# A graph layer on one core: the turn back of a chunk as a product with two stacked identities, one Vector step on GpSimd, and a new order of all work

## The chip, the cores and the metric

One core of a Trainium2 chip runs the kernel. The metric is the device time of one execution in microseconds; the engines are PE (TensorE), DVE (VectorE), ACT (ScalarE), POOL (GpSimd) and SP (SyncE), which issues the loads here. Six runs of the kernel before have a median of 193.21 us (192.71 to 194.0).

## The reference, cut to what matters

```python
h = relu(layernorm(x))                       # x: 4096 x 64
support = h @ weight                         # 64 x 64
mask = (adj != 0)                            # adj: 4096 x 4096, float32, 64 MiB
rank = cumsum(mask, axis=1); deg = rank[:, -1:]
k = minimum(deg, 100); pos = rank - (deg - k)
w = mask * where(pos > 0, 0.5 ** (k - pos), 0)
out = x + w @ support + bias
```

In each row the last 100 neighbours count, and a neighbour weighs half as much for each further neighbour that stands to the right of it.

## The kernel before, in words

The 32 row tiles (128 rows each) are taken in 8 chunks of four. Each chunk is two units: the right half of its columns first, then the left half. So there are 16 units (0 to 15) of four tiles, 64 tiles (0 to 63), and each tile is one load of 1 MB into one of 8 buffers (`a_sb`, issued by SP on line 120). Load n waits for the conversion of tile n-8, which frees its buffer.

For each tile: `convert` (line 341, DVE) turns floats to bytes; for the tiles in the tuple `signed` it is done on ACT instead (line 339). `transpose` (line 352, PE) makes four 128x128 transposes, and `settle` (line 363, DVE) copies them out of PSUM into the unit's mask. For each unit: `totals` (line 369, PE) counts bits; `split` (line 379, ACT) and `divide` (line 382, DVE) each take one byte plane of the counts out of PSUM; `carry` (line 388, POOL, units with an odd number only) brings over the count of the unit to the right; `suffix` (line 396, PE) and `clamp` (line 400, DVE) make the number of later neighbours. Then for each half of the unit's eight blocks, `place` (lines 407 and 412, PE) makes exponents in four PSUM banks out of five; `weigh` (line 420, ACT) takes the exponential of one block, and `aggregate` (line 457, PE) multiplies it with the support, which is held as a rounded part and a remainder, side by side in 64 + 64 columns (`hr`). So the accumulator `acc` has 128 partitions, 64 for either part.

Three late blocks, called `QUICK`, (14, 4), (15, 0) and (15, 4), pass by ACT: `encode` (line 426, DVE) makes an exponent code out of PSUM, `cut` (line 431, DVE) adds a constant to it, `take` (line 435, DVE) rounds it into the weight, and `gather` is their `aggregate`, with a scaled copy of the support that `lower` (line 443, POOL) has made. The last three blocks of unit 15 are weighed and multiplied in two halves (`PARTED`).

At the end of a chunk: `drain` (line 473, ACT) brings `acc` to SBUF and adds the bias; `turn_back` (line 480, PE) transposes it in four 128x128 pieces into the PSUM tile `po`; `finish` (lines 487 and 488, DVE) adds first the one 64-column part and then the other to x. The last chunk does this in two halves, with the second drain on DVE (line 471). Stores follow, on SP (lines 490 and 495) and one on ACT's queue.

The order of the work is written by a planner (lines 531 to 655): each step is a task with an engine, a rank (a place in the stream plus the numbers of `shift` and `own`), a booked cost and the tasks that it needs. The planner picks the task with the lowest rank among those that can start within `wait` of the earliest, and the steps are then issued in the order of their planned starts. Every engine keeps that order, which is fixed in the program (lines 666 to 672). The semaphores between engines follow from the data alone.

Of the kernel before, what the change touches and what calls it, by code (L numbers as in the profile page):

```python
# [31 lines left out]
def kernel(  # L32
# [134 lines left out]
    nc.vector.memset(less, 0.0)  # L167
    ones = setup.tile([P, H], F32, name="ones")
# [159 lines left out]
    low, codes, masks, words, wts, accs, tots, pts, sums8, behind, vs, signed = {}, {}, {}, {}, {}, {}, {}, {}, {}, {}, {}, (2, 8)  # L328
# [100 lines left out]
    def cut(u, k):  # L429

        nc.vector.tensor_scalar(codes[u, k][:, 1].bitcast(I32), codes[u, k][:, 0].bitcast(I32), 100 * 2.0 ** 23, None, op0=ALU.add)
# [43 lines left out]
    def turn_back(g, part=None):  # L475
        if ("o", g) not in pts:
            pts["o", g] = ps_t.tile([P, TG, 2, D], F32, tag="t", name="po")
        n = TG if part is None else TG // 2
        for tt in range(n):
            nc.tensor.transpose(pts["o", g][:, (part or 0) * n + tt, :, :].rearrange("p s d -> p (s d)"),  # L480
                                sums[g, part][:, tt * P:(tt + 1) * P], ident)

    def finish(g, part=None):
        r = slice(0, TG) if part is None else slice(part * TG // 2, (part + 1) * TG // 2)
        t = slice(g * TG % HT + r.start, g * TG % HT + r.stop)
        o = xr[:, g * TG // HT, t, :]
        nc.vector.tensor_add(o, pts["o", g][:, r, 0, :], o)
        nc.vector.tensor_add(o, pts["o", g][:, r, 1, :], o)
        if part is not None:
            (nc.sync if part else nc.scalar).dma_start(out_v[:, g * TG // HT, t, :], o)  # L490

    def store(r):
# [8 lines left out]
    shift = {"aggregate": 45, "carry": -26.5, "center": 25, "clamp": -23.5, "constants": 43.5, "convert": 36, "cut": 18.5,  # L501
             "divide": 0.5, "drain": -44.5, "encode": -1, "finish": -29.5, "first": -47.5, "halved": 5, "lower": 10.5,
             "order_of": 19.5, "power": -19.5, "relu": 39.5, "root": 26.5, "scale": 31, "second": 23.5, "settle": -26,
             "split": -38.5, "spread": 12, "square": 48.5, "store": 8, "suffix": 25, "support": 70, "take": -12, "totals": -32,
             "transpose": -15.5, "turn": 20, "turn_back": 62, "turned": 29, "weigh": 24}
    own = {
           "aggregate": {(0, 0): 6, (0, 3): -2, (0, 4): -16, (0, 6): -11, (1, 0): 7, (1, 1): -18, (1, 5): -5, (1, 7): -9, (11, 4): 10, (11, 5): 14, (11, 6): 6, (11, 7): -1, (12, 0): -20, (12, 3): 4, (12, 4): -2, (12, 5): -4, (12, 6): -10, (13, 1): -10, (13, 2): 6, (13, 3): 8, (13, 4): 1, (13, 5): -12, (13, 6): -4, (13, 7): -12, (14, 0): 2, (14, 1): 1, (14, 2): -16, (14, 3): -11, (14, 4): 15, (14, 5): -8, (14, 6): 18, (14, 7): -36, (15, 2): -4, (15, 3): -2, (15, 4): 1, (15, 5): 1, (15, 5, 0): -1, (15, 5, 1): -6, (15, 6): 8, (15, 6, 0): 7, (15, 6, 1): -3, (15, 7): -2, (2, 1): 4},
           "carry": {(1,): -2, (13,): 6, (15,): 3, (3,): 29}, "center": {(0,): 1, (1,): 2, (2,): 1, (3,): 3},
           "clamp": {(0,): -13, (1,): -8, (13,): 7, (15,): -14, (2,): -8, (3,): -2}, "constants": {(0,): -17, (1,): 15},
           "convert": {(1,): 20, (12,): -12, (13,): 4, (14,): -4, (16,): 19, (17,): 8, (18,): -16, (19,): -4, (2,): -9, (20,): -1, (4,): 5, (5,): 9, (57,): -16, (58,): -5, (59,): 8, (6,): -1, (60,): -5, (61,): -1, (7,): 1, (8,): 16, (9,): 8},  # L510
           "count": {(2,): 1}, "counted": {(2,): -18, (4,): 8}, "cut": {(14, 4): 15},
           "divide": {(0,): 24, (1,): 2, (14,): 8, (15,): -14, (2,): 15, (3,): -4},
           "drain": {(0,): 8, (5,): -22, (6,): 6, (7, 0): 7, (7, 1): 4}, "encode": {(14, 4): -9},
           "finish": {(5,): 7, (6,): -33, (7, 0): 4, (7, 1): -1}, "first": {(0, 0): -1, (1, 0): 1, (1, 1): 8},
           "halved": {(0,): -3, (1,): -5, (13,): 4, (14,): -9, (2,): 4}, "lower": {(15, 0): -3}, "order_of": {(2,): 4, (4,): 3},
           "place": {(0, 0): -8, (0, 1): -8, (1, 0): -13, (12, 1): 1, (13, 0): 8, (13, 1): -2, (14, 0): -9, (14, 1): 5, (15, 0): -26, (15, 1): 2, (2, 0): -4, (2, 1): 16},
           "power": {(): -23}, "relu": {(0,): -4, (1,): -3, (2,): 8}, "root": {(): -7}, "scale": {(3,): -6},
           "second": {(0, 0): -6, (0, 1): -1, (1, 1): 22},
           "settle": {(1,): -4, (10,): 2, (11,): 1, (12,): -9, (13,): 19, (15,): 2, (17,): -2, (18,): -19, (19,): -6, (2,): -11, (3,): 6, (4,): -11, (5,): -4, (56,): 5, (57,): 22, (58,): -2, (59,): 5, (6,): 1, (61,): -4, (63,): -4, (9,): 1},
           "split": {(0,): 5, (1,): -9, (13,): 3, (14,): 9, (15,): 3, (2,): -1, (3,): -12},  # L520
           "spread": {(0,): 10, (1,): 14, (2,): -9, (3,): -1}, "square": {(1,): 10, (2,): -5, (3,): -12},
           "store": {(0,): -13, (1,): -3}, "suffix": {(1,): 3, (13,): -36, (14,): -6, (15,): -1}, "support": {(0,): -3, (2,): 15},
           "take": {(15, 0): -4, (15, 4): -2},
           "totals": {(0,): -1, (1,): -4, (13,): 3, (14,): -4, (15,): 10, (2,): -2, (3,): 7, (4,): -15},
           "transpose": {(0, 0, 2): 4, (0, 2, 4): -9, (1, 0, 2): -8, (10, 0, 2): -16, (11, 0, 2): 7, (11, 2, 4): 14, (12, 0, 2): -2, (12, 2, 4): -18, (13, 0, 2): -1, (13, 2, 4): 4, (14, 0, 2): -16, (15, 0, 2): -1, (15, 2, 4): 5, (16, 2, 4): -14, (17, 0, 2): -12, (18, 0, 2): 29, (18, 2, 4): 29, (19, 0, 2): 16, (19, 2, 4): -4, (2, 0, 2): -2, (2, 2, 4): 1, (3, 2, 4): -15, (4, 0, 2): 3, (4, 2, 4): 21, (5, 0, 2): -4, (5, 2, 4): -4, (56, 0, 2): 1, (56, 2, 4): -1, (57, 0, 2): -27, (58, 0, 2): 1, (58, 2, 4): 8, (59, 0, 2): 5, (6, 0, 2): 25, (6, 2, 4): 37, (60, 2, 4): -7, (61, 0, 2): 10, (61, 2, 4): 6, (63, 0, 2): -8, (7, 0, 2): -2, (8, 0, 2): -1, (8, 2, 4): -16, (9, 2, 4): -1},
           "turn": {(0, 0): -12, (0, 12): 10, (0, 4): 2, (0, 8): 3, (1, 0): -25, (1, 4): -16},
           "turn_back": {(5,): 4, (6,): -22, (7, 0): 8}, "turned": {(0, 0): 2, (0, 12): 6, (1, 12): -6, (1, 4): 12, (1, 8): 14},
           "weigh": {(0, 2): 8, (0, 3): 3, (0, 4): 3, (0, 5): 4, (0, 7): -16, (1, 0): 22, (1, 3): -3, (1, 4): 1, (1, 7): 2, (12, 3): 8, (12, 4): -8, (12, 5): -6, (12, 6): -22, (12, 7): 6, (13, 0): 2, (13, 1): -12, (13, 2): 23, (13, 5): 10, (13, 6): -8, (13, 7): 5, (14, 3): -3, (14, 5): -4, (14, 7): -8, (15, 2): -4, (15, 3): -11, (15, 5, 0): 3, (15, 5, 1): -19, (15, 6): 7, (15, 6, 0): -3, (15, 6, 1): -4, (15, 7): -5, (15, 7, 0): 4, (15, 7, 1): 3, (2, 0): 2, (2, 1): 4, (2, 3): -7, (2, 4): 8, (2, 6): 2, (2, 7): -1, (3, 0): -4, (3, 1): 1}}
# [50 lines left out]
    for u, (g, c0, cb) in enumerate(UNITS):  # L579
# [3 lines left out]
        task(divide, (u,), DVE, at - 2.5, 600, 720, [("totals", u)])  # L583
# [5 lines left out]
        for k in range(2 * cb):  # L589
# [7 lines left out]
            if (u, k) in QUICK:  # L597
                weighs = "take"
                task(encode, (u, k), DVE, due - 8, 1150, 1270, [("place", u, k // 4), ("convert", NT - 2)])
                task(cut, (u, k), DVE, due - 8, 650, 770, [("encode", u, k)])  # L600
                task(take, (u, k), DVE, due - 8, 650, 770, [("cut", u, k)], ("w", ("gather", u, k)))
# [5 lines left out]
        for part in range(2 if u == U - 1 else 0):  # L607
            for k in PARTED:
                due = at + k + part
                task(weigh, (u, k, part), ACT, due + 2.5, 520, 650, [("place", u, k // 4)], None if part else ("w", ("aggregate", u, k, 1)))  # L610
                task(aggregate, (u, k, part), PE, due + 14, 260, 500, [("weigh", u, k, part)])
        if c0 == 0:
            at = POS[(u + 1) * TG]
            if u < U - 1:
                task(drain, (g,), ACT, at, 560, 620, [("aggregate", u, 2 * cb - 1)] + ([("turn_back", g - 1)] if g else []))
                task(turn_back, (g,), PE, at + 5, 440, 660, [("drain", g)], ("t", ("finish", g)))
                task(finish, (g,), DVE, at + 2, 820, 880, [("turn_back", g)])
            else:
                for part in range(2):
                    task(drain, (g, part), DVE if part else ACT, at, 300, 350, [("aggregate", u, PARTED[-1], part), *(("gather", *uk) for uk in QUICK)])  # L620
                    task(turn_back, (g, part), PE, at + 5, 220, 440, [("drain", g, part)])
# [79 lines left out]
```

## Time and profile before

| | us |
|---|---|
| median of six runs | 193.21 |
| the profiled execution | 193.93 |
| its span, first to last instruction | 192.2 |
| busy: PE, DVE, ACT, POOL | 173.1, 165.8, 158.1, 19.7 |
| landing of the last load (tile 63) | 167.76 |
| convert of tile 63 | 169.66 to 171.04 |
| first `weigh` of unit 15 | 179.50 |
| last `aggregate` ends | 186.73 |
| last store is issued | 189.56 |

The span is counted from the first instruction; what lies around it in this execution is 1.7 us. The view of the stretches gives each engine's busy time in a part of the span; the timeline gives single instructions with start, duration and, in brackets, the idle time before them and who ended it. "DVE L363" is an instruction of line 363 on DVE. Busy PE time is modelled from pipelined matmuls and overstates PE. DVE and ACT instructions in a row overlap by about 0.1 us, so one `convert` of 1.39 us takes 1.27 us of a queue that is full, and one `weigh` of 1.12 us takes 1.02.

### The profile page before, as it was taken

How to read it: one execution, taken by the hardware profiler on the slowest of the kernel's cores; microseconds unless marked ns; L12 is line 12 of the kernel's file. 1: busy time of each engine (PE TensorE's matmuls, PEld its weight loads, DVE VectorE, ACT ScalarE, POOL GpSimd, SP SyncE). 2: the span in 40 equal slices, each digit the busy share in tenths (PEclk: the TensorE clock that was granted, in tenths of full speed). 3: DMA queues.
4: the chain of work that ended last, by engine and by line, in shares of the span. 5: the costliest groups of instructions: out<-in, count | busy, mean ns of one | idle time of the engine just before them, and what ended most of it. 6: DMA issues, size and time to landing. Idle time of an engine off the chain costs nothing.

```text
span 192.2 us, 3811 instructions
## 1 busy us (share of the span) xinstructions
PE 173.1 (90%) x1504; PEld 107.1 (56%) x1504; DVE 165.8 (86%) x225; ACT 158.1 (82%) x175; POOL 19.7 (10%) x60
## 2 busy tenths in 40 slices
PE   7699998787997999999999989999999898989981
PEld 5577958353664556555665645655565454544460
DVE  4853876999998999899989988999999999988753
ACT  2289109999798799979996999999999699998880
POOL 7000053100001000100010002000100048001000
PEclk9999759997999999999999999999999999999996
DMA  6999999999999999999999999999999999602000
GB/s 218 419 421 419 419 424 421 418 416 416 426 411 424 421 418 423 423 414 426 419 414 423 423 418 419 426 414 423 414 419 418 423 419 419 270 6 82 0 3 27
DMA packets 10338, 69.49 MB, mean 362 GB/s; under 512 B 1360, under 2 KB 1616, under 8 KB 2128
## 3 DMA queue, kind: packets, MB, share of 16 engines
q1 hardware_dynamic: 10016, 69.15, 87.0%
q8 instruction: 12, 0.20, 0.4%
q10 hardware_dynamic: 304, 0.10, 0.2%
q14 instruction: 6, 0.05, 0.1%
HBM read 68.19 MB, written 1.05 MB: 360 GB/s over the span
## 4 chain that ended last, share of the span: by engine, by line
PE 43%; DVE 19%; issue 16%; ACT 13%; POOL 7%; POOLq 0%; ACTq 0%; DVEq 0%
PE acc L457 15%; ACT wk L420 11%; PE pt L352 8%; DVE m L341 8%; PE v L412 4%; DVE mt L363 4%; PE v L407 3%; PE tot L369 3%; POOL low L443 3%; PE pd L281 2%; PE pc L265 2%; PE ps L396 2%; PE px L256 2%; DVE sums L382 1%; DVE xs L307 1%
## 5 line engine op out<-in xcount | busy, mean ns | idle before, releaser
L420 ACT ACTIVATE wk<-v,floor 128x1024 fp32r<-128x1024 uint8 (+1 forms) x128 | 130.1, 1100 | 14.7 <-PE v L412 14.5
L341 DVE TENSOR_SCALAR m<-a_sb 128x2048 uint8<-128x2048 f32 x62 | 86.3, 1394 | 2.5 <-DMA a_sb<-in_adj_dram 2.5
L457 PE MATMUL acc<-wk,hr 128*128 128x512 f32 (+1 forms) x256 | 79.4, 425 | 1.5 <-ACT acc_sb L473 0.9
L457 PEld LDWEIGHTS acc<-wk,hr 128*128 128x128 f32 x256 | 43.8, 191 | 15.0 <-issue 3.4
L352 PE MATMUL pt<-ident,m 128*128 128x128 f32 x256 | 42.4, 287 | 6.7 <-DVE m L341 2.6
L363 DVE COPY mt<-pt 128x512 uint32<-128x512 uint32 x62 | 42.3, 683 | 5.9 <-PE pt L352 5.8
L352 PEld LDWEIGHTS pt<-ident,m 128*128 128x128 f32 x256 | 28.8, 144 | 24.4 <-issue 6.9
L388 POOL COPY sums<-behind 1x512 f16<-1x512 f16 x8 | 6.1, 768 | 134.4 <-ACT sums L379 134.4
L407 PE MATMUL v<-behind,where 32*128 32x512 f16 x128 | 15.1, 397 | 1.2 <-DVE behind L400 0.6
L412 PE MATMUL v<-mt,tri 32*32 32x512 f16 x512 | 14.7, 408 | 0.0
L379 ACT ACTIVATE sums<-tot 128x512 f16<-128x512 uint8 x16 | 9.6, 599 | 5.2 <-DVE sums L382 2.6
L382 DVE CAST sums<-tot 128x512 f16<-128x512 uint8 x16 | 11.0, 685 | 2.3 <-ACT sums L379 1.6
L400 DVE TENSOR_SCALAR behind<-ps,excess 128x512 f16<-128x512 f32 x16 | 11.9, 745 | 0.9 <-PE ps L396 0.8
L396 PE MATMUL ps<-sums,later 128*128 128x512 f16 x32 | 10.2, 402 | 0.7 <-POOL sums L388 0.7
L369 PE MATMUL tot<-mt,band 128*32 128x512 f16 x128 | 10.2, 395 | 0.0
L412 PEld LDWEIGHTS <-tri 32*32 32x32 f16 x512 | 4.4, 88 | 10.2 <-issue 10.2
L407 PEld LDWEIGHTS <-where 32*128 32x128 f16 x128 | 3.7, 91 | 10.7 <-issue 10.7
L248 PE MATMUL none<-junk 128*128 128x256 bf16 x49 | 7.6, 322 | 1.1 <-DVE junk L133 1.1
L260 ACT ACTIVATE mt<-px 64x512 f32<-64x512 f32 x8 | 4.2, 586 | 4.8 <-PE px L256 4.8
L248 PEld LDWEIGHTS <-junk 128*128 128x128 bf16 x49 | 5.6, 116 | 3.0 <-DVE junk L133 1.1
L473 ACT ACTIVATE acc_sb<-acc,bias_sb 128x512 f32<-128x512 f32 (+1 forms) x8 | 5.3, 664 | 1.5 <-PE acc L457 1.4
L480 PE MATMUL po<-ident,acc_sb 128*128 128x128 f32 x30 | 4.8, 280 | 1.4 <-ACT acc_sb L473 1.4
(88 smaller groups left out, 98.4 us busy)
## 6 DMA issues: line engine op xcount, KB each, us to landing
a_sb<-in_adj_dram SPq DMA_DIRECT2D x64, 1024.0 KB, 14.2
xr<-in_x_dram SPq DMA_DIRECT2D x2, 512.0 KB, 6.2
out_dram<-xr SPq DMA_DIRECT2D x1, 512.0 KB, 16.9
out_dram<-xr SPq DMA_DIRECT2D x1, 384.0 KB, 2.3
out_dram<-xr ACTq DMA_DIRECT2D x1, 64.0 KB, 1.6
out_dram<-xr SPq DMA_DIRECT2D x1, 64.0 KB, 1.6
w<-in_L_gnn_weight_dram ACTq DMA_DIRECT2D x2, 16.0 KB, 5.8
bias_sb<-in_L_gnn_bias_dram SPq DMA_DIRECT2D x1, 0.2 KB, 14.8
```

The lines of the kernel that those rows point to most:

```text
L248: nc.tensor.matmul(none[:, :2 * P], junk[:, :P], junk, start=True, stop=True)
L341: nc.vector.tensor_scalar(m_v, a_v, 0.0, 64.0, op0=ALU.not_equal, op1=ALU.add)
L352: nc.tensor.transpose(pts[n][:, c, :], m32[:, c * P:(c + 1) * P], ident)
L363: nc.vector.tensor_copy(mw, pt)
L369: nc.tensor.matmul(tot[SUB * c:SUB * (c + 1), :], band[:, SUB - 12 - 4 * a:2 * SUB - 12 - 4 * a], masks[u][:, c, :, a], start=(a == 0), st ...
L382: nc.vector.tensor_copy(*bytes_of(u, 1))
L396: nc.tensor.matmul(px, later[cb][:r, f, :], sums[:r, f, :], start=(f == 0), stop=(f == 1))
L400: nc.vector.tensor_scalar(behind[u], pts.pop((u, "s")), excess[UNITS[u][2]], float(MAX_NEIGH), op0=ALU.subtract, op1=ALU.min)
L407: nc.tensor.matmul(v, where[q, a, :], behind[u][q, :], start=True, stop=False, skip_group_check=True)
L412: nc.tensor.matmul(vs[u, 4 * a + j][SUB * c:SUB * (c + 1), :], tri[q, q], m, start=False, stop=True, skip_group_check=True)
L420: nc.scalar.activation(wts[u, k][:, :, r], v.bitcast(U8).rearrange("p (i f) -> p f i", f=4)[:, :2, r], AF.Exp, scale=-LN2, bias=floor)
L457: nc.tensor.matmul(accs[g][:, r], parts.rearrange("p s d -> p (s d)"), wk[:, s, r], start=(k == s == 0 and c0 + cb * E * P == N), stop=(c0 ...
```

## The change

`turn_back` no longer transposes. It multiplies each 128-row piece with `both`, two 64x64 identities one above the other, so that the product is the transposed sum of the two parts: 64 columns instead of 128, in an ordinary float32 product. `finish` is then one addition. `cut` goes from DVE to POOL. Tile 9 and tile 15 are converted on ACT, tile 8 no longer is. For the planner, `divide` now follows `split`, some booked costs and `wait` change, and all ranks are new.

```diff
+    both = const.tile([P, D], F32, name="both")
+    nc.vector.tensor_add(both, ident[:, :D], ident[:, D:])
...
-    low, codes, ..., signed = {}, {}, ..., (2, 8)
+    low, codes, ..., signed = {}, {}, ..., (2, 9, 15)
...
     def cut(u, k):
-        nc.vector.tensor_scalar(codes[u, k][:, 1].bitcast(I32), codes[u, k][:, 0].bitcast(I32), 100 * 2.0 ** 23, None, op0=ALU.add)
+        nc.gpsimd.tensor_scalar(codes[u, k][:, 1].bitcast(I32), codes[u, k][:, 0].bitcast(I32), 100 * 2.0 ** 23, None, op0=ALU.add)
...
     def turn_back(g, part=None):
         if ("o", g) not in pts:
-            pts["o", g] = ps_t.tile([P, TG, 2, D], F32, tag="t", name="po")
+            pts["o", g] = ps_t.tile([P, TG, 2 * D], F32, tag="t", name="po")
         n = TG if part is None else TG // 2
         for tt in range(n):
-            nc.tensor.transpose(pts["o", g][:, (part or 0) * n + tt, :, :].rearrange("p s d -> p (s d)"),
-                                sums[g, part][:, tt * P:(tt + 1) * P], ident)
+            nc.tensor.matmul(pts["o", g][:, (part or 0) * n + tt, :D], sums[g, part][:, tt * P:(tt + 1) * P], both, start=True, stop=True)
     def finish(g, part=None):
...
-        nc.vector.tensor_add(o, pts["o", g][:, r, 0, :], o)
-        nc.vector.tensor_add(o, pts["o", g][:, r, 1, :], o)
+        nc.vector.tensor_add(o, pts["o", g][:, r, :D], o)
...
-        task(divide, (u,), DVE, at - 2.5, 600, 720, [("totals", u)])
+        task(divide, (u,), DVE, at - 2.5, 610, 730, [("split", u)])
...
-                task(cut, (u, k), DVE, due - 8, 650, 770, [("encode", u, k)])
+                task(cut, (u, k), POOL, due - 8, 1800, 1900, [("encode", u, k)])
...
-                task(turn_back, (g,), PE, at + 5, 440, 660, [("drain", g)], ("t", ("finish", g)))
-                task(finish, (g,), DVE, at + 2, 820, 880, [("turn_back", g)])
+                task(turn_back, (g,), PE, at + 5, 860, 1080, [("drain", g)], ("t", ("finish", g)))
+                task(finish, (g,), DVE, at + 2, 420, 480, [("turn_back", g)])
...
-    wait = 250, 60, 250, 60, 0
+    wait = 400, 150, 600, 60, 0
...
-            lag += 1400 if key == ("load", 6) else 0
+            lag += 1400 if key in (("load", 6), ("load", 54)) else 0
```

`shift` and `own` (the ranks) differ in nearly every entry. In the built program the steps around the end stand in this order:

| engine | before | after |
|---|---|---|
| PE | turn_back 6, aggregate (14,0), totals 15, place (14,1), aggregate (14,1), (14,2), suffix 15, aggregate (14,3), (14,5), (14,6), place (15,0), gather (14,4), aggregate (14,7), (15,1), place (15,1), gather (15,0), ... gather (15,4), aggregate (15,6), (15,7) of the second half | turn_back 6, totals 15, aggregate (14,0), place (14,1), aggregate (14,1), suffix 15, aggregate (14,2), (14,3), (14,5), place (15,0), aggregate (14,6), (14,7), gather (14,4), aggregate (15,1), place (15,1), ... gather (15,0), ... aggregate (15,7) of the second half, gather (15,4) |
| DVE | settle 62, settle 63, finish 6, divide 15, encode (14,4), cut, clamp 15, take (14,4), encode (15,0), cut, take, encode (15,4), cut, take | settle 62, settle 63, finish 6, divide 15, encode (14,4), clamp 15, take (14,4), encode (15,0), encode (15,4), take (15,0), take (15,4) |
| ACT | weigh (14,0), (14,1), drain 6, weigh (14,2), (14,3), split 15, weigh (14,5) to (14,7), (15,1) ... | weigh (14,0), drain 6, weigh (14,1), (14,2), split 15, weigh (14,3), (14,5) to (14,7), (15,1) ... |
| POOL | carry 13, six `lower`, carry 15 | carry 13, six `lower`, carry 15, three `cut` |

Earlier, ACT converts tile 9 behind weigh (0,5), and tile 15 behind weigh (1,7), followed by drain 0 ahead of weigh (2,0).

## The prediction

> **What bounds the kernel now.** I read the page first, then the stretches, then the timeline of the end. The page:
>
> ```profile
> span 192.2 us, 3811 instructions
> PE 173.1 (90%) x1504; PEld 107.1 (56%) x1504; DVE 165.8 (86%) x225; ACT 158.1 (82%) x175; POOL 19.7 (10%) x60
> ...
> DVE  4853876999998999899989988999999999988753
> ACT  2289109999798799979996999999999699998880
> ...
> DMA  6999999999999999999999999999999999602000
> GB/s 218 419 421 419 419 424 421 418 416 416 426 411 424 421 418 423 423 414 426 419 414 423 423 418 419 426 414 423 414 419 418 423 419 419 270 6 82 0 3 27
> ```
>
> The loads run at 420 GB/s without a break; in the landing records they arrive every 2.49 us, the last at 167.76. No engine can shorten that. What can be shortened is the 24.4 us from there to the end of the span. DVE has no slack beside the loads:
>
> ```profile
> 90.00:120.00 30.00, 28.06 (x260) 16.92 (x258) 27.68 (x35) 28.07 (x31) 1.69 (x2) 1.00 1.01 421
> 120.00:150.00 30.00, 29.06 (x262) 17.10 (x259) 28.98 (x35) 27.85 (x30) 0.60 (x1) 1.00 1.01 419
> 163.00:171.00 8.00, 7.99 (x79) 4.65 (x78) 8.00 (x10) 7.73 (x10) 0.00 (x0) 1.00 0.46 187
> ```
>
> Columns: stretch, length, then busy time of PE, weight loads, DVE, ACT and POOL. DVE is busy 28.98 of 30 us, so it never catches up. From the landing of a unit's last tile to its `convert` pass 5.2 us in unit 3, 4.3 in unit 8, 4.9 in unit 12, and (the loads paused 1.4 us at tile 54) 2.6, 2.8 and 1.9 in units 13 to 15. ACT follows: a unit's first `weigh` comes 16.2 us after that landing in unit 3, 13.6 in unit 11, 11.7 in unit 15. The end:
>
> ```profile
> 169.66 1.39 DVE L341 TENSOR_SCALAR m<-a_sb 128x2048 uint8<-128x2048 f32 x1
> ...
> 173.75 0.64 PE L369 MATMUL tot<-mt,band 128*32 128x512 f16 x8
> ...
> 174.50 0.69 DVE L382 CAST sums<-tot 128x512 f16<-128x512 uint8 x1 [0.23 <-PE tot L369]
> ...
> 175.23 0.60 ACT L379 ACTIVATE sums<-tot 128x512 f16<-128x512 uint8 x1 [0.57 <-DVE sums L382]
> ...
> 175.89 0.60 POOL L388 COPY sums<-behind 1x512 f16<-1x512 f16 x1 [13.06 <-ACT sums L379]
> ...
> 179.50 6.67 ACT L420 ACTIVATE wk<-v,floor 128x1024 fp32r<-128x1024 uint8 x9 [0.66 <-PE v L412]
> ...
> 183.76 0.69 DVE L431 TENSOR_SCALAR code<-code 128x1024 int32<-128x1024 int32 x1
> ```
>
> Convert 63 starts 1.9 us late; `divide`, `split` and `carry` run one behind another (174.50 to 176.49); then nine weighs of unit 15 fill ACT for 6.67 us. Call their start T (179.50 now). The last product ends at T + 7.23, the last store is issued 2.83 later.
>
> **The change, part by part.**
>
> *DVE.* A `finish` costs 0.82 us of queue and will cost 0.40: six chunks before unit 13's tiles are through give 2.5 us. One more tile on ACT (9 and 15 instead of 8) gives 1.27. Together 3.8 us, against lags of 2.6 to 1.9: DVE then waits for loads. I let convert 63 start 0.4 after its landing, at 168.2, 1.5 earlier. The three cuts take 0.69 each off DVE, all in the end.
>
> *ACT.* The extra convert costs 2.5 us (the two now last 2.49 and 2.54), and it stands before unit 2's weighs, which I expect about 3.4 us later than now. ACT must win this back. A unit needs eight weighs of 1.02, a split of 0.6 and half a drain, 9.1 us, of the loads' 9.95. I book 0.3 of waiting per unit and let it be level by unit 13.
>
> *PE.* The four transposes of a chunk take 0.44 us in the chain of work. Float32 products run as two passes: `pd` on line 281 has eight records, 2 columns wide, in 0.79, and `pp` on line 304 sixteen, 128 wide, in 2.05. So four 64-wide products cost between 0.79 and 1.03, 0.35 to 0.6 more per chunk. PE waits more than that per chunk in the stretches (1 to 2 us of 30, with pipelined matmuls overstated), so the seven inner ones are hidden; uncovered, they would cost up to 4 us.
>
> *The byte planes.* `divide` behind `split` lets `carry` run beside `divide`: 0.07 + 0.60 + 0.05 + 0.69 instead of 1.99, about 0.6 less in an odd unit.
>
> *The walk to T.* Convert 63 at 168.2 to 169.6; its transposes and `settle` as now 1.5 later, 171.1; `turn_back` 6 stands ahead of `totals` and runs while PE waits; `totals` to 171.8. ACT meets `split` behind weigh (14,2): with weigh (14,0) at 168.6 (now 169.95), three weighs and a drain of 0.58 make 172.3. Split to 172.9, four weighs to 177.0, T = 177.1. The other way: divide to 173.6, encode to 174.8, clamp to 175.5, and `place` needs the bank of weigh (14,6), free at 175.9; ready at 176.7. So T comes 2.4 us earlier.
>
> *Behind T: the cut on POOL.* encode (15,4) starts at T + 3.0 as now and takes 1.23; cut c, take 0.70, 0.2 between, the unqueued product 0.74. The end is T + 5.95 + c, where now it is T + 7.23. The trace has no 1024-wide POOL step. Its rows:
>
> ```profile
> L388 POOL COPY sums<-behind 1x512 f16<-1x512 f16 x8 | 6.1, 768 | 134.4 <-ACT sums L379 134.4
> L443 POOL TENSOR_SCALAR low<-hr 128x128 fp32r<-128x128 f32 x6 | 5.2, 890 | 0.0
> L298 POOL TENSOR_SCALAR t<-t 128x32 f32<-128x32 f32 x3 | 0.9, 290 | 0.3
> ```
>
> The copy is 0.60 when undisturbed, so 1024 at that rate take 1.2, the low bound. TENSOR_SCALAR takes 0.29 at 32 wide and 0.52 (median) at 128, 2.4 ns per element, so 2.7 at 1024, the high bound. I take 1.9, the middle: the kind is that of the second, but its rows are so short that fixed cost weighs in the slope. It makes +0.6. At 1.2 it adds nothing. At 2.7 take (14,4), which stands ahead of encode (15,0), also holds back encode (15,0) and so `place` (15,1) by c - 2.1 = 0.6, and the cost is 2.0.
>
> [...]
>
> While POOL ran `low`, a convert took 1.75 instead of 1.39 and two `low` took about 1.6 instead of 0.52. [...]
>
> *The last stage.* Two halves: each `turn_back` 0.2 longer, each `finish` 0.32 shorter (0.29 + 0.03): -0.24.
>
> **Sum.** -2.4 + 0.6 - 0.24 = -2.0. The profiled execution took 193.93, so 191.9; it was one of the slower of six. From the median of 193.21: **191.2**.
>
> **The rivals.**
> 1. *ACT stays the bound* (no change). For: from 161 to 186.2 ACT idles only 1.5 us, and it gets 2.5 us more work. Against: it idles 0.3 to 1.4 us at most first weighs from 52 to 151. If weigh (14,0) stays at 169.95, T is 178.5: -1.0 + 0.6 - 0.24, 192.6; if ACT ends 1 us later still, 193.6.
> 2. *POOL's cut is the new wait* (slower). Place: encode (15,4) to take (15,4), and take (14,4) ahead of encode (15,0). The sum is zero where 2c + 3.85 - 7.23 = 2.64, c = 3.0. For: the slow `low` records have 1.1 more than the others, which on 2.7 gives 3.8. There the cost is 4.2 and the time 194.8. Against: an idle DVE then, and the copy row.
> 3. *The product does not do what it says*: DVE gains, but `turn_back` 6 at 1.0 and more, ahead of `totals` 15, puts PE late. If its drain comes 1 us late, T moves by 1: 192.2.
> 4. *All goes well*: T = 176.0 (landing plus the bare chain), c up to 1.2: -3.7, 189.5.
>
> **How the numbers follow.** Forecast with 3 and 4 (189.5 to 192.2): 0.62. Rival 1 and the cut near 2.7 (192.2 to 194.0): 0.22. Rival 2: 0.16. Range 189.5 to 193.9, which takes in both bounds of c and rival 1 and leaves out most of rival 2. A difference of 0.5% (192.24 and 194.18) is about what a measurement of this kernel can tell from no change. Faster 0.62, same 0.22, slower 0.16.
>
> **What would show it.** In the profile after: last landing still near 167.8; convert 63 within 0.5 of it; `split` 15 ahead of `divide`; first weigh of unit 15 near 177; line 433's POOL rows near 1.9; one addition of 0.43 in `finish`; `turn_back` of eight records in 0.8 to 1.0. I am wrong if T is near 179 (ACT), if c is over 2.7, or if the loads pause for want of buffers, which moves the landing itself.

## The result and the profile after

The changed kernel takes **194.35 us** (median of 21 runs, 193.46 to 195.59); the kernel before, on the same chips, 192.83 (42 runs, 191.9 to 194.0). The ratio is 1.0079, interval 1.0061 to 1.0097: slower by 0.8%. The forecast was 191.2, faster, with a range up to 193.9. The profiled execution of the changed kernel took 194.45.

The page of the changed kernel, against the lines shown of before:

```profile
span 192.7 us, 3898 instructions
PE 176.5 (92%) x1535; PEld 113.0 (59%) x1535; DVE 160.7 (83%) x213; ACT 160.0 (83%) x176; POOL 28.2 (15%) x63
...
DVE  4863885999989999999999999998999799965632
ACT  2379225897999999999998999999989998799820
POOL 7000074010001000000100010001000091015740
PEclk9999958999999999999999999999999999999968
```

DVE has lost 5.1 us of work and POOL has got 8.5 more. The last six digits are the stage to look at: DVE falls to 5 and 6 there, POOL rises to 5 and 7, and PE's clock shows a 6 in the last slice but one. The end in single instructions (the timeline; start, duration, engine, line; in brackets the idle time before and who ended it):

```profile
168.22 1.38 DVE L343 TENSOR_SCALAR m<-a_sb 128x2048 uint8<-128x2048 f32 x1
...
172.26 0.61 ACT L381 ACTIVATE sums<-tot 128x512 f16<-128x512 uint8 x1
...
172.91 0.69 DVE L384 CAST sums<-tot 128x512 f16<-128x512 uint8 x1 [0.91 <-ACT sums L381]
172.94 0.60 POOL L390 COPY sums<-behind 1x512 f16<-1x512 f16 x1 [13.07 <-ACT sums L381]
...
174.86 2.78 POOL L433 TENSOR_SCALAR code<-code 128x1024 int32<-128x1024 int32 x1 [1.33 <-DVE code L428]
...
176.87 3.12 ACT L422 ACTIVATE wk<-v,floor 128x1024 fp32r<-128x1024 uint8 x3
...
177.67 0.69 DVE L437 CAST wk<-code 128x1024 fp32r<-128x1024 f32 x1 [2.24 <-POOL code L433]
178.28 1.22 DVE L428 TENSOR_SCALAR code<-v 128x1024 int32<-128x1024 uint8 x1
179.58 5.50 POOL L433 TENSOR_SCALAR code<-code 128x1024 int32<-128x1024 int32 x2 [1.94 <-DVE code L428]
...
182.39 1.51 DVE L437 CAST wk<-code 128x1024 fp32r<-128x1024 f32 x1 [0.75 <-POOL code L433]
183.96 1.22 PE L459 MATMUL acc<-wk,low 128*128 128x512 f32 x2 [1.63 <-DVE wk L437]
...
185.12 0.69 DVE L437 CAST wk<-code 128x1024 fp32r<-128x1024 f32 x1 [1.22 <-POOL code L433]
186.68 0.96 PE L459 MATMUL acc<-wk,low 128*128 128x512 f32 x2
187.68 0.47 ACT L475 ACTIVATE acc_sb<-acc,bias_sb 128x256 f32<-128x256 f32 x1 [3.60 <-PE acc L459]
```

First read down to 172.94: convert 63 starts 0.21 behind its landing (168.01), where it was 1.90 (this delay is called its lag below); the split comes before the divide, and the carry runs beside the divide. T, the first weigh of unit 15, is 176.87 in this trace (the weighs are shown from there; ACT has no pause before them). All of that is the forecast. Then read the three cuts on POOL: 2.78, and two in 5.50. The take of (14, 4) waits 2.24 for the first; encode (15, 0) stands behind that take and starts at 178.28, though its `place` had ended at 176.69; the third cut starts 0.68 after its encode ended (the first 0.08), because the second still runs; the last take waits 1.22 for it. The last product ends at 187.64, T + 10.8, where it was T + 7.23.

The stretches show a second cost. Columns: stretch, length, busy PE, weight loads, DVE, ACT, POOL, granted clock of PE:

```profile
180.57:183.98 3.41, 1.71 (x9) 1.00 (x7) 2.58 (x2) 3.41 (x6) 3.41 (x2) 1.00 0.00 0
183.98:187.39 3.41, 3.41 (x12) 2.84 (x12) 0.69 (x1) 0.10 (x1) 1.11 (x1) 0.50 0.00 0
```

PE has little to do while gather (15, 0) waits for its weight, and the halved blocks stand behind that gather in PE's queue. Then its clock is 0.50 for 3.41 us; in it the eight halved products take 1.91 us, where experiment 4 shows them at 1.09 at a clock of 1.00, and the last product takes 0.96 instead of 0.73. The last weight is ready at 185.81, and its product, 0.74 when nothing is in front of it, ends 1.83 later.

### The profile page after: what moved, and what is told of

It reads as the page before. It is cut to its first block, busy times and chain, and to the rows that moved or that the text cites. A ratio compares the mean times of both kernels' runs of the same rounds, so it can differ in the third digit from the quotient of the medians.

```text
span 192.7 us, 3898 instructions
## 1 busy us (share of the span) xinstructions
PE 176.5 (92%) x1535; PEld 113.0 (59%) x1535; DVE 160.7 (83%) x213; ACT 160.0 (83%) x176; POOL 28.2 (15%) x63
## 5 line engine op out<-in xcount | busy, mean ns | idle before, releaser
L343 DVE TENSOR_SCALAR m<-a_sb 128x2048 uint8<-128x2048 f32 x61 | 84.3, 1390 | 2.5 <-DMA a_sb<-in_adj_dram 2.4
L459 PE MATMUL acc<-wk,hr 128*128 128x512 f32 (+1 forms) x256 | 77.1, 422 | 0.9 <-ACT wk L422 0.4
L459 PEld LDWEIGHTS acc<-wk,hr 128*128 128x128 f32 x256 | 44.4, 194 | 14.7 <-issue 5.1
L365 DVE COPY mt<-pt 128x512 uint32<-128x512 uint32 x61 | 41.6, 682 | 5.0 <-PE pt L354 4.6
L390 POOL COPY sums<-behind 1x512 f16<-1x512 f16 x8 | 5.0, 628 | 131.6 <-ACT sums L381 131.6
L482 PE MATMUL po<-both,acc_sb 128*128 128x64 f32 x60 | 8.1, 277 | 1.4 <-ACT acc_sb L475 1.4
L250 PE MATMUL none<-junk 128*128 128x256 bf16 x48 | 8.3, 350 | 1.1 <-DVE junk L133 1.1
L482 PEld LDWEIGHTS po<-both,acc_sb 128*128 128x128 f32 x60 | 7.3, 192 | 3.1 <-ACT acc_sb L475 3.0
L433 POOL TENSOR_SCALAR code<-code 128x1024 int32<-128x1024 int32 x3 | 8.3, 2772 | 3.3 <-DVE code L428 3.3
```

Source lines behind the costliest of these rows:

```text
L343: nc.vector.tensor_scalar(m_v, a_v, 0.0, 64.0, op0=ALU.not_equal, op1=ALU.add)
L365: nc.vector.tensor_copy(mw, pt)
L433: nc.gpsimd.tensor_scalar(codes[u, k][:, 1].bitcast(I32), codes[u, k][:, 0].bitcast(I32), 100 * 2.0 ** 23, None, op0=ALU.add)
L459: nc.tensor.matmul(accs[g][:, r], parts.rearrange("p s d -> p (s d)"), wk[:, s, r], start=(k == s == 0 and c0 + cb * E * P == N), stop=(c0 ...
L482: nc.tensor.matmul(pts["o", g][:, (part or 0) * n + tt, :D], sums[g, part][:, tt * P:(tt + 1) * P], both, start=True, stop=True)
```

## The experiments

The first theory was that the whole loss is the cut on POOL, while the product gives a gain by the time it saves on DVE. Against it stood that the new order or the added work on ACT loses, whatever the cut does; and later, that the product's gain is there only in an order that hands it on. In the expectations the theories have letters, each with the time it expects.

**1. The changed kernel with the cut on DVE.** Nothing else is changed, the order neither.

```diff
-        nc.gpsimd.tensor_scalar(codes[u, k][:, 1]...
+        nc.vector.tensor_scalar(codes[u, k][:, 1]...
```

> The changed kernel with the cut back on VectorE and nothing else changed: every other step keeps its place in the order. Theory A (the three GpSimd cuts of 2.77 us, one behind another on that engine, hold the last product): in the changed kernel the first weigh of unit 15 starts at 176.87 and the last product ends at 187.64; with cuts of 0.69 on VectorE the weighs decide again and the last product ends 7.2 us after that start, at 184.1, so the run is about 3.5 us shorter, near 190.8, some 1% below the kernel before. Theory B (the float32 product of the turn back and its double number of PE records cost the time): nothing but a few tenths comes back, 194. Theory C (the new order is the worse one, whoever cuts): the first weigh of unit 15 is no earlier than in the changed kernel and the time stays over 193.

191.34 (ratio to before 0.9923, 0.9894 to 0.9953), 0.5 over the time that theory A expected. So in this order the cut on POOL costs 3.0 us, and the rest of the change is worth 1.5. The timeline of this kernel's end:

```profile
176.53 6.68 ACT L422 ACTIVATE wk<-v,floor 128x1024 fp32r<-128x1024 uint8 x9
...
181.27 0.69 DVE L433 TENSOR_SCALAR code<-code 128x1024 int32<-128x1024 int32 x1
...
182.06 0.69 DVE L437 CAST wk<-code 128x1024 fp32r<-128x1024 f32 x1
183.59 0.63 PE L459 MATMUL acc<-wk,low 128*128 128x512 f32 x2
184.26 0.47 ACT L475 ACTIVATE acc_sb<-acc,bias_sb 128x256 f32<-128x256 f32 x1 [1.06 <-PE acc L459]
```

T is 176.53, the last weight is ready at 182.75, and now it waits: its product stands last in PE's queue, behind the halved blocks, and ends at T + 7.7, not at T + 6.6, where the prediction's T + 5.95 + c puts it for c = 0.69.

**2. The kernel before with the cut on POOL**, the same edit the other way round.

```diff
-        nc.vector.tensor_scalar(codes[u, k][:, 1]...
+        nc.gpsimd.tensor_scalar(codes[u, k][:, 1]...
```

> The kernel before with the cut on GpSimd and nothing else changed. Theory A: the first weigh of unit 15 stays at 179.5; take (14,4) ends near 180.0 instead of 178.5, and since take (15,0) stands ahead of encode (15,4) here, the second and the third cut cannot overlap with anything: the last product ends near 190.5 instead of 186.7, and the time is 3.8 us longer, up to 1 us more if PE loses its clock while it waits, 196.5 to 197.5. Theories B and C: the cut alone is worth under 1 us, below 194.

197.66 (1.0245, 1.0215 to 1.0276), 4.8 more than before and 0.2 over the expected range. The cut takes 2.77 here too. The take of (14, 4) waits 1.37 us for it, and the two later takes wait 2.9 us each:

```profile
183.61 0.69 DVE L435 CAST wk<-code 128x1024 fp32r<-128x1024 f32 x1 [2.89 <-POOL code L431]
...
188.33 0.69 DVE L435 CAST wk<-code 128x1024 fp32r<-128x1024 f32 x1 [2.88 <-POOL code L431]
```

PE's clock is 0.50 again, from 185.14 for 3.41 us. The price of the cut depends on the order: 4.8 in the old one, 3.0 in the new one.

**3. The planner told the true price.** The changed kernel, where the booked cost of a cut is what the trace shows. Encode (15, 0) then moves ahead of take (14, 4), and gather (14, 4) behind place (15, 1).

```diff
-                task(cut, (u, k), POOL, due - 8, 1800, 1900, [("encode", u, k)])
+                task(cut, (u, k), POOL, due - 8, 2770, 2870, [("encode", u, k)])
```

> The changed kernel, with the planner's booked cost of a cut at the measured 2.77 us instead of 1.80. The planner then puts encode (15,0) ahead of take (14,4), and the product of (14,4) behind place (15,1); nothing else moves. Theory A in its finer form (half of the loss is that take (14,4) holds back encode (15,0), and the second cut holds the third): encode (15,0) starts near 176.8 instead of 178.3, the third cut ends near 184.1 instead of 185.1, the last product near 185.7 to 186.5 instead of 187.6: 192.4 to 193.2. If the waits on GpSimd do not matter (B, C): no change, 194.3.

192.45 (0.9973, 0.9955 to 0.9992). Of the 3.0 us, 1.9 are due to the order that the wrong price made. PE keeps its clock here (the eight halved products take 1.11 us, where the changed kernel has 1.91 at a clock of 0.50), so what the halved clock costs (experiment 4) is among the 1.9. What is left to experiment 1, 1.1 us, goes with the cut's length; the two orders differ too, so it isn't that alone. The two later cuts:

```profile
177.88 5.89 POOL L433 TENSOR_SCALAR code<-code 128x1024 int32<-128x1024 int32 x2 [0.44 <-DVE code L428]
```

**4. PE kept busy.** The changed kernel with twelve products that nobody uses ahead of gather (15, 0), for the clock alone.

```diff
     def gather(u, k):
...
+        if (u, k) == (U - 1, 0):
+            idle = ps_v.tile([P, W], F32, tag="v", name="idle")
+            for i in range(12):
+                nc.tensor.matmul(idle[:, :2 * P], junk[:, :P], junk, start=True, stop=True)
```

> The changed kernel with twelve matrix products on zeros (their results are not used) ahead of the product of block (15,0), where PE stands idle for 1.63 us. In the stretch from 184 to 186 the granted clock of the changed kernel is 0.50 and its half-size products take 0.43 us in a row instead of 0.2. Theory D (the low clock behind that wait is part of the loss): with the zeros the clock stays at 1.0, the half-size products are done by 185.3 and the last product ends near 186.6 instead of 187.6, 193.4. If the clock does not follow from the idle time, or the last take is what decides: 194.3.

193.50 (1.0034, 1.0014 to 1.0054), 0.85 less than the changed kernel. The clock is 1.00 throughout, and the halves and the last product are at their old durations:

```profile
181.98 1.49 PE L466 MATMUL idle<-junk 128*128 128x256 bf16 x12
...
184.35 1.09 PE L459 MATMUL acc<-wk,hr 128*128 128x256 f32 x8
...
185.69 0.73 PE L459 MATMUL acc<-wk,low 128*128 128x512 f32 x2 [0.25 <-DVE wk L437]
```

**5. The product taken back.** Experiment 1 with the four transposes and the two additions of before; the order stays the new one.

```diff
-            nc.tensor.matmul(pts["o", g][:, (part or 0) * n + tt, :D], sums[g, part][...], both, start=True, stop=True)
+            nc.tensor.transpose(pts["o", g][:, (part or 0) * n + tt, :, :].rearrange("p s d -> p (s d)"), sums[g, part][...], ident)
```

> The first experiment's kernel (cut on VectorE, all else as changed) with the turn back as transposes and two additions again. Theory A (the additions saved, 0.42 us in each of the six chunks ahead of unit 14, are what lets VectorE reach the loads): VectorE is up to 2.5 us later again, convert 63 starts 1.2 to 2 us behind its landing instead of 0.15, the first weigh of unit 15 comes 0.8 to 1.5 us later than 176.5, and the last stage is 0.5 longer: 192.6 to 193.3. Theory E (the new order and the serial byte planes give the gain, the additions fill VectorE's waits): the first weigh stays near 176.5, only the last stage costs: 191.8.

193.51 (1.0031, 1.001 to 1.0053), 2.2 more than experiment 1 and 0.2 over the expected range. The last load lands at 168.15, and convert 63 is 2.46 late again:

```profile
170.61 1.38 DVE L343 TENSOR_SCALAR m<-a_sb 128x2048 uint8<-128x2048 f32 x1
...
179.26 6.68 ACT L422 ACTIVATE wk<-v,floor 128x1024 fp32r<-128x1024 uint8 x9
```

T is 11.1 us behind the landing where it was 8.8. A part of this lag may belong to the execution and not to the kernel. It took 194.05, while four of the twelve took 192.65 to 192.73, 1.3 to 1.4 over the median of experiment 1; and PE's clock from 20 to 35 us was 0.66 in it, 0.77 in the profiled execution of experiment 1.

**6. Tile 15 back on DVE.** Experiment 1 with only the first two tiles of `signed` on ACT (2 and 9); the same edit stands in `settle`.

```diff
-        if n in signed:
+        if n in signed[:2]:
```

> The first experiment's kernel with tile 15 converted on VectorE (tile 9 alone remains an ACT tile besides 2). Theory A: VectorE is 1.27 us later from unit 4 on and makes it up by unit 12, where the changed kernel waits for loads; ACT is 2.5 us earlier in unit 2, which it also would have made up: convert 63 within 0.5 us of its landing, within 0.5 us of 191.3. If VectorE has nothing to spare up to the end: 1.27 us later, 192.5.

191.53 (0.9937, 0.9914 to 0.996). That is 0.2 more than experiment 1, and the intervals overlap: not measurable here. In the two traces the lag of convert 63 is 0.32 against 0.15.

**7. The cut on DVE, and planned there.** The changed kernel with the edit of experiment 1 and the cost that the kernel before books.

```diff
-                task(cut, (u, k), POOL, due - 8, 1800, 1900, [("encode", u, k)])
+                task(cut, (u, k), DVE, due - 8, 650, 770, [("encode", u, k)])
```

> The changed kernel with cut on VectorE in the planner too, at 0.65 us. In the order this puts the product of (15,4) ahead of the last two half products, cut (15,0) and take (15,0) ahead of encode (15,4), and the product of (14,4) ahead of two others. In the first experiment the last product, that of (15,4), ends 0.46 us behind the half products, though its weight is ready 0.8 us earlier: theory A expects these 0.4 to 0.5 us back, 190.9. If ACT's last weigh decides: 0.2 or less.

190.97 (0.9901, 0.9881 to 0.9922), the best of all kernels tried. With each place of the cut planned at its own price (this kernel and experiment 3), the move to POOL costs 1.5 us. The product of (15, 4) now stands ahead of the last two halved blocks, and the last product ends at T + 7.24.

**8. The new order alone.** Experiments 5 and 6 together: transposes, two additions, the cut on DVE, as many tiles on ACT as before.

> The new order with none of the other parts: cut on VectorE, transposes with two additions, tile 15 on VectorE (tile 9 on ACT where the kernel before has tile 8). Theory A (relief of VectorE gives the gain): VectorE is as loaded as in the kernel before, convert 63 starts 1.5 to 3 us behind its landing, the first weigh of unit 15 between 178 and 179.5, the time 192.3 to 193.2, the kernel before's. Theory E (order): first weigh before 177.3 and the time 191.8 or less.

193.55 (1.0026, 1.0006 to 1.0046), 0.3 over the expected range. The order gives nothing by itself; it loses about 0.5. Convert 63 is 2.35 late in the profiled execution, where PE's clock from 20 to 35 us is 0.66 as in experiment 5.

**9. The product alone, in the old order.** The kernel before with `both`, the product and the single addition.

> The kernel before with the product of two identities and the single addition, in its old order, nothing else changed (cut on VectorE, tiles 2 and 8 on ACT, divide ahead of split where the old order has it). Theory A (relief of VectorE is the gain, the product brings it): the five experiments so far put 2.2 us on the product in the new order, and the new order without it at 0.5 us over the kernel before; in the old order it should bring 1.5 to 2.2 as well, 190.8 to 191.5. Theory E in its remaining form (the product pays only in an order that is made for it): VectorE spends the time saved in waits, 192.2 or more, with the first weigh of unit 15 later than 178.5.

193.40 (1.0032, 1.0004 to 1.0061). No gain: the theory by which the product gains by itself (190.8 to 191.5) falls, and the one by which the order has to hand the gain on is left. There is none although the profiled execution has convert 63 only 0.5 behind its landing. Its timeline says where the time stays:

```profile
171.21 1.10 PE L482 MATMUL po<-both,acc_sb 128*128 128x64 f32 x8 [0.86 <-ACT acc_sb L475]
...
172.77 0.63 PE L371 MATMUL tot<-mt,band 128*32 128x512 f16 x8
...
173.52 0.69 DVE L384 CAST sums<-tot 128x512 f16<-128x512 uint8 x1 [0.74 <-PE tot L371]
...
178.53 6.68 ACT L422 ACTIVATE wk<-v,floor 128x1024 fp32r<-128x1024 uint8 x9 [0.67 <-PE v L414]
```

`settle` 63 ended at 171.08, but `totals` 15 has to let `turn_back` 6 pass, which waited for its drain until 171.21, and then aggregate (14, 0). In the changed kernel `totals` 15 starts at 171.47, right behind a `turn_back` 6 that had started at 170.43.

**10. The same kernel again**, for a second profiled execution.

> The kernel before with the product, a second time, for another profile: the profiled execution of the first time took 192.69, the shortest of its twelve (median 193.40). If the profile was an odd one, this one's first weigh of unit 15 lies later than 178.43, at 179 or more, with the median again near 193.4 (theory E: the old order does not hand the time on). If the median was the odd one, it comes near 192 now (theory A).

193.31 (1.0032, 0.9998 to 1.0067). This profiled execution took 195.03, with convert 63 2.86 late. At unit 4 its lag was already 6.04, against 3.75 in the execution of experiment 9; 1.5 of this difference was there at unit 1. It arises in the first 60 us. PE's clock from 7 to 20 us was 0.87 in it, 1.00 in experiment 9, and from 40 to 60 us 0.91 against 1.00.

**11. The old order with `totals` 15 first.** Experiment 9, where `totals` 15 goes ahead of `turn_back` 6 and aggregate (14, 0), and `finish` 6 behind encode (14, 4).

```diff
-    for at, _, f, args in sorted(order, key=lambda o: o[:2]):
+    order.sort(key=lambda o: o[:2])
+    for key, ahead in ((("turn_back", 6), ("totals", 15)), (("aggregate", 14, 0), ("turn_back", 6)), (("finish", 6), ("encode", 14, 4))):
...
+        order.insert(n + 1, (order[n][0], *moved[1:]))
+    for at, _, f, args in order:
```

> The kernel before with the product, in the old order but for the end: totals 15 stands ahead of turn_back 6 and aggregate (14,0) on PE, finish 6 behind encode (14,4) on DVE. In the profile of the kernel before with the product, settle 63 ends at 171.08, but totals 15 ends only at 173.41, since turn_back 6 waits for drain 6 until 171.21 and aggregate (14,0) follows. If that is where the old order loses the gain, totals 15 ends near 171.8, the byte planes follow at 172 to 173.7, the first weigh of unit 15 comes 0.8 to 1.2 us earlier, and the time falls by as much against the kernel before with the product of this call. If the loss lies earlier (ACT late from the middle on): no change.

194.05 (1.005, 1.0018 to 1.0082). The store of chunk 6 now leaves before `finish` 6, so this kernel's output lacks the neighbours' sum in that chunk; no step is left out. The profiled execution, 194.54, has the large lag of experiment 10, and beside that one T is 180.36 instead of 180.85: a gain of 0.5, where 0.8 to 1.2 were expected. The median does not show it: half of these twelve runs were at 194.5 or more, three of ten in experiment 10.

**12 to 14. The kernel before, three more executions with a profile.**

> The kernel before, unchanged, one more profile. If its executions differ in the first 30 us as those of the kernel with the product do, then in an execution near 192 convert 63 starts 0.3 to 1 us behind its landing instead of 1.9, the first weigh of unit 15 comes 10.5 to 11 us behind that landing instead of 11.7, and the lag is already smaller at unit 4. If they do not, the lag is 1.9 again whatever the time.

> The same, a second look: an execution near 194 is to show the lag of 1.9 us or more and a first weigh 11.7 us or more behind the landing, one near 192 the smaller one.

> The same, a third look: time and lag of convert 63 go together, about 1 us for 1 us.

| execution of before | convert 63 behind its landing | T behind the landing | clock of PE from 40 to 60 us |
|---|---|---|---|
| 193.93 (the profile above) | 1.90 | 11.74 | 0.91 |
| 193.34 | 1.36 | 11.19 | 0.91 |
| 192.79 | 0.94 | 10.77 | 1.00 |
| 192.52 | 0.57 | 10.41 | 1.00 |

Lag and time go together, one to one. The execution of 192.52 is the partner for experiment 9, which has the same lag (0.5). Here PE turns the chunk back in

```profile
171.28 0.66 PE L480 MATMUL po<-ident,acc_sb 128*128 128x128 f32 x4 [0.87 <-ACT acc_sb L473]
...
172.33 0.64 PE L369 MATMUL tot<-mt,band 128*32 128x512 f16 x8
...
178.09 6.68 ACT L420 ACTIVATE wk<-v,floor 128x1024 fp32r<-128x1024 uint8 x9 [0.66 <-PE v L412]
```

that is, 0.44 less than the product's 1.10, and `totals` 15 is 0.44 earlier (172.33 against 172.77), T too (178.09 against 178.53). The product wins 0.21 back between the last product and the last store's issue (2.62 against 2.83). At nearly equal lag the longer `turn_back` ahead of `totals` 15 takes more in the old order than the saved addition brings there.

## Why the prediction was wrong

**Right, up to T.** Convert 63 at 0.21 behind its landing (0.4 said); ACT 3.5 us late at the first weigh of unit 2 (3.4 said) and level again near unit 8 (unit 13 said); the carry beside the divide; `turn_back` in eight records, though `turn_back` 6 takes 1.11 us (0.8 to 1.0 said); T at 176.87 (177.1 said). Rival 1, that ACT stays the bound, and rival 3, that `turn_back` 6 comes late, did not happen in this order; the place that rival 3 names is where the old one loses 0.44 us with the product (experiment 9).

**The step that failed** is the way from T to the last product, T + 5.95 + c: its term "I take 1.9, the middle" was too small, and what the cuts do to each other, to encode (15, 0) at this length and to PE's clock stood in its sum at 1.9 as nothing. It said T + 7.85, and the trace shows T + 10.77. The cut takes 2.77 (0.69 on DVE), just over the 2.7 that the prediction named as a sign of being wrong. The two ends were 1.2 (from the copy's row) and 2.7 (from the slope of POOL's own TENSOR_SCALAR rows, 2.4 ns per element). The second was the same operation on the same engine, and it was right to 3%; the reason for doubting it, that its rows are short, did not hold. By the price that the prediction gave for 2.7 (2.0 in place of 0.6) its own sum would have been -0.6, so 193.3 from the profile's 193.93 and 192.6 from the median, inside what it called no change: the price of the cut alone does not make the kernel slower.

**What was missed besides.** In the two profiled executions the sum reads so: forecast 191.9, measured 194.45, 2.55 more. T gives -0.2, the last stage -0.3, what lies behind the last store's issue +0.1, and the way from T to the last product +2.9 (T + 10.77 against T + 7.85). Of these 2.9, 0.9 is c itself (2.77 - 1.9). Encode (15, 4) comes at T + 3.54, not T + 3.0: 0.5, the hold-back of encode (15, 0), which the prediction priced in its upper bound. The third cut waits 0.6 for the second on POOL (0.68 less the usual 0.08): the prediction looked at who waits for a cut on DVE, and not at the cuts' own queue. And the last product ends 1.83 behind its weight, not 0.74: 1.1, most of it PE's halved clock, which experiment 4 prices at 0.85 in the medians (and 1.04 in the traces, T + 9.73 against T + 10.77). These four make 3.1, within 0.2 of the 2.9; of this 0.08 is a slip of the prediction, whose terms of T + 5.95 + c add up to T + 5.87 + c.

**Rival 2 is what happened**, in the place it named (encode (15, 4) to take (15, 4), and take (14, 4) ahead of encode (15, 0)). But its point of decision, c = 3.0, was too high, because that sum has neither POOL's queue nor PE's clock in it. At 2.77 the kernel was already slower by 1.5.

**"The unqueued product 0.74"** failed too, more quietly. Even with a cut of 0.69 the last product stands behind the halved blocks and ends at T + 7.7 (experiment 1). Experiment 7, planned with the cut on DVE, has it at T + 7.24. So the low end of c would have given less than the sum said; this is worked out from the two orders and was not run with such a cut.

**The price in the order.** The prediction took the planned order as given. Experiment 3 shows that the 1800 booked in it is itself a cause: with 2770 booked, 1.9 of the 3.0 us come back with the cut still on POOL.

**The basis.** The profile of before was one of its longer executions: a lag of 1.9, where the execution of 192.79, at the median, has 0.94. The prediction counted 1.5 us for bringing the lag to 0.4, which from such an execution brings 0.5, and took off the 0.72 between profile and median as well. The changed kernel's profile lies at its median, so this makes some 0.6 of the miss of 3.15 (191.2 to 194.35); the other 2.55 are the terms above.

**Where the gain comes from.** Experiments 1, 5, 8 and 9 together: in the medians the product is worth 2.2 us in the new order and nothing in the old one, and the new order is worth nothing without it. The traces show how this is put together. T is the last landing, plus the lag of convert 63, plus the way from there to T:

| kernels | lag of convert 63 | convert 63 to T |
|---|---|---|
| old order, transposes (before, four executions; experiment 2) | 0.57 to 1.90 | 9.83 to 9.84 |
| old order, product (experiments 9 and 10) | 0.50 and 2.86 | 10.34 |
| the same with `totals` 15 first (experiment 11) | 3.01 | 9.83 |
| new order, transposes (experiments 5 and 8) | 2.46 and 2.35 | 8.65 and 8.67 |
| new order, product (the changed kernel, experiments 1, 3, 4, 6, 7) | 0.15 to 0.32 | 8.65 to 8.67 |

The new order shortens the way by 1.2 us, with the product or without it. Without the product it loses as much in the lag; with it the lag is small in all six traces. In the old order the product makes the way 0.5 longer, and the two traces do not show that the relief of DVE makes the lag smaller. Which part of the new order lets the relief through is not shown: `totals` 15 ahead of `turn_back` 6 alone does not (experiment 11). How much of the 2.2 is the product and how much the clock of the first 35 us, which was lower in the traces of experiments 5 and 8 (0.66 from 20 to 35 us, 0.77 in experiment 1), is not separated; by the shortest run of either (192.65 and 190.91) it is 1.7. The tile on ACT, booked at 1.27 us of DVE's queue, shows 0.2, which is not clear of noise.

**The last stage.** From the last product to the last store's issue it takes 2.30 instead of 2.83: -0.53, not -0.24. The second half of `turn_back` no longer waits for the `finish` of the first: the halves run from 188.20 and 188.72, and both additions follow together (189.42 to 189.91). That is the new order's doing, which the prediction left out. With the product in the old order the stage takes 2.62, and with the new order without the product 2.73 (experiments 9 and 5).

**Open.** What sets the lag of an execution in the first 60 us. PE's clock in that time goes with it: in the old order the lag is 0.50 to 0.94 in the three executions with no dip from 40 to 60 us (0.57, 0.94, and 0.50 in experiment 9), 1.36 and 1.90 with one (0.91), and 2.86 and 3.01 in experiments 10 and 11, where the clock was also 0.87 from 7 to 20 us. Which of the two is the cause was not tried, since nothing moved the clock alone. The medians of experiments 9 to 11 mix executions with small and large lags, so a difference of some 0.3 us between them is not read.

## What to carry to other kernels

When an operation moves to an engine that has rows of the same operation, extrapolate these rows, however short, before those of a lighter one; and count the queue of the receiving engine as well as those who wait for it. Where an order is planned from booked costs, a wrong cost is paid twice, once as length and once in the order: measure the step, put the number in, and plan again. Take the basis of a sum from an execution near the median, since a lag that only the profiled execution has is no gain to be won.

## What the runs showed of the hardware

- The 128x1024 int32 addition of `cut` took 2.77 us on POOL (the changed kernel) and 0.69 on DVE (the kernel before, experiment 1), a quarter of that.
- Of a cut on POOL and a take on DVE that overlapped in these traces, the one that started later was slowed: a take that started less than 0.1 us behind a cut took 1.51 instead of 0.69 in the changed kernel (182.39) and in experiments 3 and 4, and the cut kept its 2.77; in experiment 3 a cut that started 0.17 us behind a take took 3.16 instead of 2.77, and the take kept its 0.69. An encode beside a cut took 1.23 (180.41 in the changed kernel), next to 1.22 without one (178.28).
- PE's clock was 0.50 from 183.98 to 187.39 in the changed kernel, 3.41 us, and 1.00 behind that. In the 3.41 us before, PE was busy for 1.71, with one idle piece of 1.63 in front of gather (15, 0). In experiment 2 it was 0.50 for 3.41 us too (185.14 to 188.55), with 1.08 busy of the 3.41 us before and 2.33 idle at a stretch. With the piece of 1.63 filled (experiment 4: 3.02 of the same 3.41 us busy) the clock stayed at 1.00. In experiment 3, where the longest piece was 0.98, the eight halved products took 1.11 us, next to 1.09 in experiment 4 at a clock of 1.00.
- The four float32 products of 64 columns of `turn_back` 6 were eight records and 1.10 us (experiment 9), its four 128-column transposes four records and 0.66 (the execution of 192.52).
